# Turns behind the LSTM layer and in the attention layer: from TensorE to 32x32 blocks on VectorE and DMAs, with a new ranking of ready operations

## The chip, the cores and the metric

The kernel runs on one core of a Trainium2 chip, as one program and one launch. The metric is the device time of that program in microseconds. The core's engines run beside each other, each in the order of its own instructions: TensorE (PE in the profile) does matrix products and 128x128 turns (transposes) into PSUM, VectorE (DVE) and ScalarE (ACT) work elementwise, GpSimd (POOL) does small per-row work, and SyncE (SP) issues DMAs. They wait for each other by semaphores.

## The reference

x has 128 batches of 64 nodes with 256 features, which are 8192 rows, all float32. Four layers follow, each as x = layernorm(x + layer(x, adj)):

- Layer 0: three graph convolutions, 256 to 512 to 1024 to 256 features, with the squared entries of adj.
- Layer 1: a spectral layer. The eigenvectors U of a normalised Laplacian turn the nodes, two small products with a relu lie between, and U turns them back.
- Layer 2: two graph convolutions, then LSTMs over windows of 1, 2, 3 and 4 nodes (p = 1 to 4), each of which overwrites the last node of its windows.
- Layer 3: attention among the 64 nodes of a batch.

```
h = x @ W + b_lin                                  # layer 3
scores = (h @ h.T) * graph                         # zeros become -1e16
out = softmax(scores, axis=2) @ h + b
x = layernorm(x + out)
```

## The kernel before

A tile is 128 rows, that is two batches. Four tiles make a group of 512 rows, and there are 16 groups, numbered 0 to 15 in the code (the listing's group variable g). Layer 0 runs first, two groups at a time, with the eigenvector computation woven in; its products are recorded at line 940 and its VectorE work at line 52. Six groups' rows stay in SBUF, ten wait in a DRAM tile called `rest` and are read back when a buffer of X comes free.

Layers 1 to 3 are run by a planner (`Plan`, line 98 on). `unit` (line 1518) notes the work of two groups, or of one for the last four (`SINGLE`), as operations with an engine, an estimated cost, and dependencies. `Plan.run` keeps up to three units going and emits, again and again, the operation that can start earliest. Among operations of one engine that can start within 0.02 us of the earliest, `rank` (line 163) decides: the lower group number goes first, and for TensorE at the very end the group with the most operations left. Emission fixes the order of PE, DVE, ACT and POOL instructions (`manual_schedule`); DMAs on SP are placed by the framework. Buffers are slots by tag: `w` (seven of 128x1024), `v`, `ps` (eight PSUM banks), `gates` and others. `MOST` (line 112) keeps some free slots of each tag for the oldest unit. All instructions that the planner emits are recorded at line 156, so the profile tells them apart by tile name only.

The steps that matter here, by function:

- `turns` (line 1202) notes 128x128 transposes on TensorE: a product with `ident` as one operand, one pass each, where a float32 matrix product makes two instructions.
- `lstm` and `four` (lines 1378 and 1502) keep the state with features on the partitions: hT, in tiles w.
- `from_lstm` (line 1294) copies hT into batch order (VectorE and ScalarE), turns it on TensorE (8 turns a group), and adds half of it to the rows xs, since hT holds twice the hidden state. `norm` (line 1232) then does the layer norm: statistics on VectorE, the inverse root on GpSimd, the scaling on VectorE (on ScalarE for the last two groups, `ENDING`).
- `layer3` (line 1306) turns xs (8 turns a group) to xT, makes hT = xT times dw with the bias dbl on ScalarE, makes the scores, turns hT back to rows hn (8 turns) and adds the bias, takes the softmax without the division, turns e (the tile att, 4 turns), and multiplies eT with hn. The division by the row sum sm comes with the residual.

```
turns([(ps[k][:, cols(t)], xs[:, t, k * P:(k + 1) * P]) for k in range(2)])         # layer3: xT
turns([(p[:, j, c * P:(c + 1) * P], hT[:, c, (t + j) * P:(t + j + 1) * P]) ...])    # layer3: hn
turns([(p[:, t * P:(t + 1) * P], e[:, t, :]) for t in range(nt)])                   # layer3: eT
```

Of the kernel before, what the change touches and what calls it, by code (L numbers as in the profile page):

```python
# [11 lines left out]
F32 = mybir.dt.float32  # L12
# [85 lines left out]


class Op:  # L100
    __slots__ = ("engine", "calls", "cost", "lag", "before", "left", "after", "tiles", "start", "group", "rank", "ready", "unit")


class Plan:
# [4 lines left out]

    LAG = {"PE": 0.205, "DVE": 0.13, "ACT": 0.14, "POOL": 0.0, "SP": 2.0}  # L110

    MOST = {"w": 4, "v": 2, "ps": 4, "gates": 2, "hs": 2}
    OWN = {"PE": 0.0, "DVE": 0.125, "ACT": 0.105, "POOL": 0.0, "SP": 0.0}

    def __init__(self, engines, place, slots):
# [42 lines left out]
    def run(self, units, ways):  # L158
# [4 lines left out]
        def rank(op):  # L163
            if op.engine == "PE" and not todo and len(left) <= LASTS:
                return -left[op.group]
            return op.group or 99

        def candidates(guard):
            oldest = min([u for u in going if u] or [0])
# [22 lines left out]
        while todo or going:  # L192
            while todo and len(going) < ways + (0 in going):
                self.unit, f = todo.pop(0)
                self.ops, self.group = [], 0
                f()
                going[self.unit] = len(self.ops)
                for op in self.ops:
                    left[op.group] = left.get(op.group, 0) + 1
                    if not op.left:  # L200
                        able[op.engine].append(op)
            t, op = (candidates(True) if todo or len(left) > LASTS else None) or candidates(False)
            e = op.engine
            for tile in op.tiles:
                if tile.real is None:
                    s = self.slots[tile.tag]
                    tile.slot, tile.unit = s.index(min(s)), op.unit
                    tile.real = self.place(tile.tag, tile.slot, tile.shape)
                    s[tile.slot] = 1e9
                    held[op.unit, tile.tag] = held.get((op.unit, tile.tag), 0) + 1  # L210
            self.emit(op)
            able[e].remove(op)
            op.start = t
            self.free[e] = t + op.cost
            end = t + op.cost + self.LAG[e]
            for tile in op.tiles:
                tile.left -= 1
                tile.until = max(tile.until, end)
                if not tile.left and tile.slot is not None:
                    self.slots[tile.tag][tile.slot] = tile.until  # L220
                    held[tile.unit, tile.tag] -= 1
            for other in op.after:
                other.ready = max(other.ready, t + op.cost + self.OWN[e] if other.engine == e else end)
                other.left -= 1
                if not other.left:
                    able[other.engine].append(other)
            going[op.unit] -= 1
            left[op.group] -= 1
            if not left[op.group]:
                del left[op.group]  # L230
            if not going[op.unit]:
                del going[op.unit]
# [512 lines left out]
CELLS = 3  # L745
OUTS = 4
LASTS = 3
SINGLE = 4

RING = 6  # L750

# [56 lines left out]
def kernel(  # L808
# [90 lines left out]
    adT2 = keep.tile([P, P], F32, name="adT2")  # L899
    nc.gpsimd.memset(adT2, 0.0)  # L900
    sqT2 = keep.tile([P, P], F32, name="sqT2")
    rs_row = keep.tile([P, P], F32, name="rs_row")
    rs_col = keep.tile([P, 1], F32, name="rs_col")
    u2 = keep.tile([P, P], F32, name="u2")
# [5 lines left out]
    cw1 = load(keep, "cw1", c_w1, "(k p) f -> p k f", [P, 2, D], p=P)  # L910
    dw = load(keep, "dw", d_w, "(k p) f -> p k f", [P, 2, D], p=P)
    dbl = load(keep, "dbl", d_bl, "p (k o) -> p k o", [P, 2, 1], o=1)
    cb1 = keep.tile([P, 2], F32, name="cb1")
    nc.sync.dma_start(cb1, c_b1)
    wide = {}
# [205 lines left out]
    pr = tl(psa, [P, 512], "ps", bufs=6)  # L1121
    PE.matmul(pr[:, :P], ones, adT2, start=True, stop=True)
    V.tensor_copy(rs_row, pr[:, :P])
    V.tensor_reduce(rs_col, adst, AX.X, ALU.add)
    V.tensor_scalar(wide["c_b0"], wide["c_b0"], rs_col, None, op0=ALU.mult)
    V.tensor_add(cbi, cbi, cbh)
    for q in (slice(0, 4), slice(6, 8)):
        V.tensor_scalar(cbi[:, :, q], cbi[:, :, q], 0.5, None, op0=ALU.mult)
    phase_a.close()
# [19 lines left out]
        nc.gpsimd.memset(att[i], 0.0)  # L1149


    def place(tag, slot, shape):
        if tag == "att":
            return att[slot][:, :shape[1], :]
        if tag == "ps":
            return tl(psb, shape, f"ps{slot}")
        if tag in ("w", "v", "gates", "c", "hs"):
# [1 line left out]
        return tl(few, shape, f"{tag}{slot}")  # L1159

    plan = Plan({"PE": nc.tensor, "DVE": nc.vector, "ACT": nc.scalar, "POOL": nc.gpsimd, "SP": nc.sync}, place,
                {"ps": 8, "w": WIDE, "v": 4, "gates": GATES, "c": CELLS, "hs": OUTS, "att": ATT, "mx": 4, "sm": 4, "st": 4, "mv": 4,
                 "rs": 4, "nm": 4})
    V, S, G, Q = (Noted(plan, e) for e in ("DVE", "ACT", "POOL", "SP"))

# [63 lines left out]
        S.copy(dst[:, 1, :], ps[1])  # L1229
        return dst  # L1230

    def norm(x, scalar):
        st, mv, rs = plan.tile("st", [P, 2, 6]), plan.tile("mv", [P, 2, 2]), plan.tile("rs", [P, 2])
        for t in range(2):
            V.bn_stats(st[:, t, :], x[:, t, :])
            V.bn_aggr(mv[:, t, :], st[:, t, :])
        G.tensor_scalar(rs, mv[:, :, 1], EPS, None, op0=ALU.add)
        G.tensor_tensor(rs, rs, half[:, :2], ALU.pow, cost=0.74)
        if scalar:
            nm = plan.tile("nm", [P, 2])  # L1240
# [9 lines left out]
    def layer1(xs):  # L1250
# [14 lines left out]
        for t in range(0, 4, 2):  # L1265
# [1 line left out]
            for j in range(2):  # L1267
                run(p[:, j, :], [(z[:, (t + j) * P:(t + j + 1) * P], bw2)])
            V.tensor_add(xs[:, t:t + 2, :], p, xs[:, t:t + 2, :])
            norm(xs[:, t:t + 2, :], False)  # L1270

    def to_lstm(xs):
        a = mixed(xs, adT2)
        g1 = as3(work(), 4)
        for t in range(0, 4, 2):
            p = ps4((P, 2, D))
# [14 lines left out]
            lstm(hT, p, first, nw)  # L1291
        return hT

    def from_lstm(xs, hT, g):
        hb = as3(work(), 2)
        for bs in (slice(0, 4), slice(4, 8)):
            for k, copy, cost in ((0, V.tensor_copy, 0.33), (1, S.copy, 0.56)):
                copy(as3(hb[:, k, :], 8)[:, bs, :], hT[:, k, :, bs].rearrange("p n b -> p b n"), cost=cost)
        for t in range(0, 4, 2):
            p = ps4((P, 2, D))  # L1300
            turns([(p[:, j, k * P:(k + 1) * P], hb[:, k, (t + j) * P:(t + j + 1) * P]) for j in range(2)
                   for k in range(2)])
            V.scalar_tensor_tensor(xs[:, t:t + 2, :], p, 0.5, xs[:, t:t + 2, :], op0=ALU.mult, op1=ALU.add)
            norm(xs[:, t:t + 2, :], g in ENDING)

    def layer3(xs, g, first, nt):

        tiles = range(first, first + nt)

        def cols(t, n=1):  # L1310
            return slice((t - first) * P, (t - first + n) * P)
# [1 line left out]
        def part(tile, a):  # L1313
            return as3(tile[:, :tile.at.size * nt // 4], a)

        xT = part(work(), 2)
        ps = [ps4() for _ in range(2)]
        for t in tiles:
            turns([(ps[k][:, cols(t)], xs[:, t, k * P:(k + 1) * P]) for k in range(2)])
        if g in ENDING:  # L1320
            S.copy(xT[:, 0, :], ps[0][:, :nt * P])
        else:
            V.tensor_copy(xT[:, 0, :], ps[0][:, :nt * P])
        S.copy(xT[:, 1, :], ps[1][:, :nt * P])
        hT = part(work(), 2)
        for c in range(2):
            p = ps4()[:, :nt * P]
            run(p, [(dw[:, k, c * P:(c + 1) * P], xT[:, k, :]) for k in range(2)])
            S.activation(hT[:, c, :], p, AF.Identity, bias=dbl[:, c, :])
        p = ps4((P, nt, N))  # L1330
        calls = []
        for t in range(nt):
# [11 lines left out]
        mx = plan.tile("mx", [P, 4])[:, :nt]  # L1344
        V.tensor_reduce(mx, s, AX.X, ALU.max)
        V.tensor_sub(s, s, mx.unsqueeze(2).to_broadcast([P, nt, N]))
        e = plan.tile("att", [P, nt, P])
        for h in range(2):
            hs = slice(h * N, (h + 1) * N)
            S.activation(e[hs, :, hs], s[hs, :, :], AF.Exp, cost=0.215 + 0.00042 * nt * N)  # L1350
        hn = part(work(), nt)
        for t in range(0, nt, 2):
            p = ps4((P, 2, D))
            turns([(p[:, j, c * P:(c + 1) * P], hT[:, c, (t + j) * P:(t + j + 1) * P]) for j in range(2)
                   for c in range(2)])

            V.tensor_add(hn[:, t:t + 2, :], p, wide["d_b"].unsqueeze(1).to_broadcast([P, 2, D]))
        sm = plan.tile("sm", [P, 4])[:, :nt]
        p = ps4()[:, :nt * P]
        turns([(p[:, t * P:(t + 1) * P], e[:, t, :]) for t in range(nt)])  # L1360
        eT = work2()[:, :nt * P]
        S.copy(eT, p)
        V.tensor_reduce(sm, e, AX.X, ALU.add)
        V.reciprocal(sm, sm)
        for t in range(0, nt, 2):
            p = ps4((P, 2, D))
            for j in range(2):
                run(p[:, j, :], [(eT[:, (t + j) * P:(t + j + 1) * P], hn[:, t + j, :])])
            x2 = xs[:, first + t:first + t + 2, :]
            for j in range(2):  # L1370
                V.scalar_tensor_tensor(x2[:, j, :], p[:, j, :], sm[:, t + j:t + j + 1], x2[:, j, :],
                                       op0=ALU.mult, op1=ALU.add)
            norm(x2, g in ENDING)
            at = 4 * g + first + t
            for j in range(2):
                Q.dma_start(out_t[:, at + j, :], x2[:, j, :])
# [171 lines left out]
    def left_over():  # L1548
        for piece in norms:
            plan.note("POOL" if piece.__name__ == "root" else "ACT", piece, 0.5, 1.5 * len(plan.ops))  # L1550

    with tc.manual_schedule(engines={mybir.EngineType.PE, mybir.EngineType.DVE, mybir.EngineType.Activation,
                                     mybir.EngineType.Pool}):
# [44 lines left out]
```

## Time and profile before

| what | value |
|---|---|
| median of 3 runs | 2458.52 us (2457.69 to 2458.81) |
| profiled execution, first to last instruction | 2455.8 us |
| between that span and the median | 2.7 us |
| TensorE busy in the 40 slices of the span | 0.9 or more in all but the last |
| granted TensorE clock, mean | 0.998 |
| DMA in the span | 42.69 MB, mean 17 GB/s |

The profiled execution has no time of its own beside its span, so the span is set against the median of the runs. Times are microseconds unless marked ns. In a line of a group the fields are: source line, engine, operation, output tile <- input tiles, shapes, count | busy us, mean ns of one | idle time of the engine in front of it, and what ended most of that. In a timeline the first two numbers are start and length of a run of equal instructions, and brackets hold the idle time before. In a line of stretches the fields are the stretch, its length, the busy time of PE, its weight loads, DVE, ACT and POOL, and then the granted TensorE clock, the DMA share and GB/s. In a line of DMA issues the last number is the median from issue to landing. An instruction's duration holds its latency: on TensorE the next one starts long before it is over, so the pitch between starts is what counts.

### The profile page before, as it was taken

The page shows a single profiled execution, that of the slowest core. Times are in us where ns is not written, and L with a number is a line of the kernel's source. Part 1 is how long each engine was busy: PE and PEld are TensorE (multiplying, and loading weights), DVE is VectorE, ACT ScalarE, POOL GpSimd, SP SyncE. Part 2 cuts the span into 40 slices and gives each one's busy share as a digit, 9 for nine tenths or more (in the row PEclk, how much of TensorE's full clock was granted, in tenths as well). Part 3 has the DMA queues.
Part 4 walks back from the last instruction along what each step waited for, and adds up shares of the span by engine and source line. Part 5 has one row for each costly group of instructions (what it writes and reads, how often), then busy time and mean ns, then how long its engine had stood idle before and what let it go on. Part 6 is the DMA issues. An engine that isn't in the chain of part 4 may idle for free.

```text
span 2455.8 us, 40814 instructions
## 1 busy us (share of the span) xinstructions
PE 2431.6 (99%) x15500; PEld 2158.3 (88%) x15500; DVE 1618.6 (66%) x5676; ACT 1073.0 (44%) x2610; POOL 137.5 (6%) x315
## 2 busy tenths in 40 slices
PE   9999999999999999999999999999999999999997
PEld 7888888878887899989989998998998998988996
DVE  6888877778888265584684486477558458374336
ACT  2333433333333354445444445444444444545555
POOL 0000000000000010010010000001001001010002
PEclk9999999999999999999999999999999999999999
DMA  7000000000000020010000001001001000000000
GB/s 227 9 1 18 9 10 10 9 10 9 9 1 1 35 87 1 1 36 1 1 18 18 1 1 35 1 1 36 1 1 35 1 1 18 1 10 1 1 1 27
DMA packets 27972, 42.69 MB, mean 17 GB/s; under 512 B 2944, under 2 KB 22144, under 8 KB 27776
## 3 DMA queue, kind: packets, MB, share of 16 engines
q1 hardware_dynamic: 27424, 39.81, 4.7%
q8 instruction: 122, 2.00, 0.3%
q14 instruction: 74, 0.61, 0.1%
q10 hardware_dynamic: 352, 0.28, 0.0%
HBM read 26.45 MB, written 13.63 MB: 16 GB/s over the span
## 4 chain that ended last, share of the span: by engine, by line
PE 94%; DVE 4%; DMA 1%; ACT 0%; issue 0%; POOL 0%; SPq 0%; ACTq 0%; POOLq 0%; DVEq 0%
PE ps L156 62%; PE ps L940 31%; DVE D L52 1%; DVE X L156 1%; PE pc L296 1%; DMA XA<-in_x_dram 1%; DVE st L156 0%; DVE tw L52 0%; POOL rs L156 0%; DVE w L156 0%; DVE h L52 0%; ACT gates L156 0%; DVE gates L156 0%; DVE u L52 0%; DVE v L156 0%
## 5 line engine op out<-in xcount | busy, mean ns | idle before, releaser
L156 PE MATMUL ps<-w,wih 128*128 128x128 f32 (+2 forms) x4144 | 752.7, 315 | 0.9 <-DVE gates L156 0.9
L156 PEld LDWEIGHTS ps<-w,wih 128*128 128x128 f32 x4144 | 646.5, 191 | 37.0 <-issue 6.7
L156 ACT ACTIVATE gates<-ps,cbi 128x168 f32<-128x168 f32 (+2 forms) x832 | 342.2, 417 | 361.2 <-PE ps L156 353.0
L156 PE MATMUL ps<-hs,whh 128*128 128x168 f32 (+1 forms) x1952 | 345.1, 291 | 0.0
L156 PEld LDWEIGHTS ps<-hs,whh 128*128 128x128 f32 x1952 | 288.9, 191 | 1.2 <-issue 1.0
L156 PE MATMUL ps<-w,sums 128*128 128x128 f32 x1776 | 237.7, 275 | 0.0
L940 PE MATMUL ps<-aw,h 128*128 128x256 f32 x1024 | 227.2, 379 | 0.0
L156 DVE SCALAR_TENSOR_TENSOR gates<-gates 128x256 f32<-128x256 f32 (+2 forms) x220 | 83.9, 382 | 215.7 <-ACT gates L156 215.1
L156 PEld LDWEIGHTS ps<-w,sums 128*128 128x128 f32 x1776 | 218.1, 192 | 1.5 <-issue 1.2
L940 PEld LDWEIGHTS ps<-aw,h 128*128 128x128 f32 x1024 | 192.9, 190 | 25.9 <-ACT h L949 0.5
L156 ACT ACTIVATE gates<-gates,cbi 128x256 f32<-128x256 f32 x272 | 116.2, 497 | 194.6 <-DVE gates L156 194.6
L949 ACT ACTIVATE h<-h 128x512 f32<-128x512 f32 x128 | 80.4, 629 | 196.3 <-DVE h L52 196.1
L156 DVE TENSOR_TENSOR gates<-gates,ps 128x256 f32<-128x256 f32 x340 | 128.4, 417 | 19.4 <-PE ps L156 14.4
L940 PE MATMUL ps<-ss,tw 128*128 128x256 f32 x512 | 117.9, 380 | 0.0
L940 PE MATMUL ps<-ss,aw 128*128 128x256 f32 x512 | 117.3, 379 | 0.0
L940 PE MATMUL ps<-m,aw 128*128 128x256 f32 x512 | 117.1, 380 | 0.0
L156 DVE SCALAR_TENSOR_TENSOR c<-gates,c 128x256 f32<-128x256 f32 (+2 forms) x156 | 57.1, 366 | 87.2 <-ACT gates L156 87.0
L940 PE MATMUL ps<-aw,m 128*128 128x512 f32 x256 | 114.6, 593 | 0.0
L156 DVE TENSOR_TENSOR gates<-v,ps 128x256 f32<-128x256 f32 x136 | 55.6, 417 | 80.7 <-ACT v L156 49.9
L940 PEld LDWEIGHTS ps<-ss,aw 128*128 128x128 f32 x512 | 96.6, 190 | 12.8
L940 PEld LDWEIGHTS ps<-ss,tw 128*128 128x128 f32 x512 | 96.3, 190 | 12.9 <-issue 0.2
L940 PEld LDWEIGHTS ps<-m,aw 128*128 128x128 f32 x512 | 95.6, 190 | 12.6 <-issue 0.5
(314 smaller groups left out, 3734.7 us busy)
## 6 DMA issues: line engine op xcount, KB each, us to landing
out_dram<-X SPq DMA_DIRECT2D x64, 128.0 KB, 1.8
rest<-XA SPq DMA_DIRECT2D x10, 512.0 KB, 2.6
X<-rest SPq DMA_DIRECT2D x10, 512.0 KB, 3.3
XA<-in_x_dram SPq DMA_DIRECT2D x18, 256.0 KB, 6.0
wih<-in_c_ih_dram SPq DMA_DIRECT2D x4, 1024.0 KB, 7.4
aw<-in_a_w_dram SPq DMA_DIRECT2D x3, 1024.0 KB, 10.8
X<-in_x_dram SPq DMA_DIRECT2D x12, 256.0 KB, 5.9
whh<-in_c_hh_dram SPq DMA_DIRECT2D x3, 1024.0 KB, 9.4
```

The lines of the kernel that those rows point to most:

```text
L52: return getattr(self.engine, name)(out, *args, **kw)
L156: getattr(e, name)(*[real(x) for x in args], **{k: real(v) for k, v in kw.items()})
L296: PE.matmul(out, lhsT, rhs, start=True, stop=True)
L940: PE.matmul(out, lhsT, rhs, start=start, stop=stop)
L949: S.activation(dst, src, AF.Relu)
```

## The change

All groups but the last two stop turning on TensorE behind layer 2 and in layer 3:

- VectorE's `transpose` turns each 32x32 block inside its own 32 partitions and writes the blocks in an order of its own. The new function `across` moves the blocks to their partitions: one DMA writes the 128x1024 tile to a DRAM tile `far` (eight slots), four DMAs read it back, each into 32 partitions.
- This is done for hT behind the LSTM (two VectorE turns a group), for xs (four), and for the hidden rows hn of layer 3 (two). The products read the result through strided views. hn is now a second ScalarE activation with the summed bias dbb = dbl + b, and no longer a biased copy of the turned hT.
- e is turned in one VectorE instruction, and eight DMAs put its blocks straight into the block-diagonal tile att. The exponential is one ScalarE instruction, and the row sum runs over 64 columns a tile and not over 128.
- The factor of a half on hT is gone. Layer 1's norm now gives rows of twice the size (`twice`), so the sum behind the LSTM is twice the old one, and its norm takes four times the eps. The first graph product of layer 2 uses adH2, half of adT2, so layer 2 sees the same values as before.
- The planner computes for each operation the chain that is left behind it in its unit (`tail`), and ranks by `due` = 30 us times the group's number, less that chain. `MOST` for w goes from 4 to 3. The pieces of the layer norms that layer 0 leaves over are chained to each other.

```
-    MOST = {"w": 4, "v": 2, "ps": 4, "gates": 2, "hs": 2}
+    MOST = {"w": 3, "v": 2, "ps": 4, "gates": 2, "hs": 2}
@@ rank
-            return op.group or 99
+            return op.due
@@ run
+                for op in reversed(self.ops):
+                    op.tail = op.cost + max([x.tail + (self.OWN if x.engine == op.engine else self.LAG)[op.engine]
+                                             for x in op.after] or [0.0])
+                    op.due = op.group * PERIOD - op.tail
...
+PERIOD = 30.0
+FARS = 8
...
+    V.tensor_scalar(adH2, adT2, 0.5, None, op0=ALU.mult)
+    V.tensor_add(dbb, dbb, dbl)
...
+    far = [aside.tile([P, 1024], F32, name=f"far{i}") for i in range(FARS)]
@@ to_lstm
-        a = mixed(xs, adT2)
+        a = mixed(xs, adH2)
+    def across(src):
...
+        far = plan.tile("far", [P, 1024])
+        Q.dma_start(far, src, cost=0.6)
+        dst = work()
+        for j in range(4):
+            Q.dma_start(dst[32 * j:32 * j + 32].rearrange("r (i f) -> r i f", i=4),
+                        seen(far[:, 256 * j:256 * j + 256], "(i r) f -> r i f", i=4), cost=0.6)
+        return dst
@@ from_lstm (the last two groups keep the turns)
+        z = work()
+        for k in range(2):
+            V.transpose(z.rearrange("p (j t k f) -> p t j k f", j=4, t=4, k=2)[:, :, :, k],
+                        hT[:, k].rearrange("p n b -> p b n"))
+        y = across(z).rearrange("p (i m f) -> p m i f", i=4, m=8)
         for t in range(0, 4, 2):
-            p = ps4((P, 2, D))
-            turns([(p[:, j, k * P:(k + 1) * P], hb[:, k, (t + j) * P:(t + j + 1) * P]) for j in range(2)
-                   for k in range(2)])
-            V.scalar_tensor_tensor(xs[:, t:t + 2, :], p, 0.5, xs[:, t:t + 2, :], op0=ALU.mult, op1=ALU.add)
-            norm(xs[:, t:t + 2, :], g in ENDING)
+            x2 = xs[:, t:t + 2, :].rearrange("p t (k i f) -> p (t k) i f", k=2, i=4)
+            V.tensor_add(x2, y[:, 2 * t:2 * t + 4], x2)
+            norm(xs[:, t:t + 2, :], False, 4 * EPS)
@@ layer3 (the last two groups keep the turns)
+            z = work()
+            for t in range(0, 4, 2):
+                for k in range(2):
+                    V.transpose(z.rearrange("p (i k t r) -> p t i k r", i=4, k=2, t=4)[:, t:t + 2, :, k],
+                                xs[:, t:t + 2, k * P:(k + 1) * P])
+            xT = across(z).rearrange("p (j k t r) -> p k t j r", j=4, k=2, t=4)
...
             S.activation(hT[:, c, :], p, AF.Identity, bias=dbl[:, c, :])
+            if not ending:
+                h = work2()
+                S.activation(h, p, AF.Identity, bias=dbb[:, c, :])
+                V.transpose(z.rearrange("p (j t c f) -> p t j c f", j=4, t=4, c=2)[:, :, :, c], h)
+        if not ending:
+            hn = across(z).rearrange("p (i t c f) -> p t c i f", i=4, t=4, c=2)
...
+            S.activation(s, s, AF.Exp)
+            V.tensor_reduce(sm, s, AX.X, ALU.add)
+            z = sc.rearrange("p a c -> p (a c)")[:, 256:]
+            V.transpose(z.rearrange("p (b t r) -> p t b r", b=2, t=4), s)
+            for h in range(2):
+                for b in range(2):
+                    for a in range(2):
+                        Q.dma_start(e[64 * h + 32 * b:64 * h + 32 * b + 32, :, 64 * h + 32 * a:64 * h + 32 * a + 32],
+                                    z[64 * h + 32 * a:64 * h + 32 * a + 32, 128 * b:128 * b + 128]
+                                    .rearrange("p (t r) -> p t r", t=4), cost=0.6)
```

More of the change, by code (lines that the diff above doesn't have):

```diff
@@ L100 @@
 class Op:
-    __slots__ = ("engine", "calls", "cost", "lag", "before", "left", "after", "tiles", "start", "group", "rank", "ready", "unit")
+    __slots__ = ("engine", "calls", "cost", "lag", "before", "left", "after", "tiles", "start", "group", "rank", "ready", "unit", "tail", "due")
 class Plan:
     LAG = {"PE": 0.205, "DVE": 0.13, "ACT": 0.14, "POOL": 0.0, "SP": 2.0}
-    MOST = {"w": 4, "v": 2, "ps": 4, "gates": 2, "hs": 2}
+    MOST = {"w": 3, "v": 2, "ps": 4, "gates": 2, "hs": 2}
     OWN = {"PE": 0.0, "DVE": 0.125, "ACT": 0.105, "POOL": 0.0, "SP": 0.0}
@@ L901 @@
     sqT2 = keep.tile([P, P], F32, name="sqT2")
+    adH2 = keep.tile([P, P], F32, name="adH2")
     rs_row = keep.tile([P, P], F32, name="rs_row")
@@ L912 @@
     dbl = load(keep, "dbl", d_bl, "p (k o) -> p k o", [P, 2, 1], o=1)
+    dbb = load(keep, "dbb", d_b, "(k p o) -> p k o", [P, 2, 1], p=P, o=1)
     cb1 = keep.tile([P, 2], F32, name="cb1")
@@ L1154, in place @@
             return att[slot][:, :shape[1], :]
+        if tag == "far":
+            return far[slot]
         if tag == "ps":
@@ L1161 @@
     plan = Plan({"PE": nc.tensor, "DVE": nc.vector, "ACT": nc.scalar, "POOL": nc.gpsimd, "SP": nc.sync}, place,
-                {"ps": 8, "w": WIDE, "v": 4, "gates": GATES, "c": CELLS, "hs": OUTS, "att": ATT, "mx": 4, "sm": 4, "st": 4, "mv": 4,
+                {"ps": 8, "w": WIDE, "v": 4, "gates": GATES, "c": CELLS, "hs": OUTS, "att": ATT, "far": FARS, "mx": 4, "sm": 4, "st": 4, "mv": 4,
                  "rs": 4, "nm": 4})
@@ L1230, in mixed, with norm @@
         return dst
-    def norm(x, scalar):
+    def norm(x, scalar, eps=EPS, twice=False):
         st, mv, rs = plan.tile("st", [P, 2, 6]), plan.tile("mv", [P, 2, 2]), plan.tile("rs", [P, 2])
@@ L1236, in norm @@
             V.bn_aggr(mv[:, t, :], st[:, t, :])
-        G.tensor_scalar(rs, mv[:, :, 1], EPS, None, op0=ALU.add)
+        if twice:
+            G.tensor_scalar(rs, mv[:, :, 1], eps, 0.25, op0=ALU.add, op1=ALU.mult)
+        else:
+            G.tensor_scalar(rs, mv[:, :, 1], eps, None, op0=ALU.add)
         G.tensor_tensor(rs, rs, half[:, :2], ALU.pow, cost=0.74)
@@ L1269, in layer1 @@
             V.tensor_add(xs[:, t:t + 2, :], p, xs[:, t:t + 2, :])
-            norm(xs[:, t:t + 2, :], False)
+            norm(xs[:, t:t + 2, :], False, twice=True)
     def to_lstm(xs):
-        a = mixed(xs, adT2)
+        a = mixed(xs, adH2)
         g1 = as3(work(), 4)
@@ L1292, in to_lstm, with seen @@
         return hT
-    def from_lstm(xs, hT, g):
[L1295 to L1298, printed above, removed]
-        for t in range(0, 4, 2):
-            p = ps4((P, 2, D))
-            turns([(p[:, j, k * P:(k + 1) * P], hb[:, k, (t + j) * P:(t + j + 1) * P]) for j in range(2)
-                   for k in range(2)])
-            V.scalar_tensor_tensor(xs[:, t:t + 2, :], p, 0.5, xs[:, t:t + 2, :], op0=ALU.mult, op1=ALU.add)
-            norm(xs[:, t:t + 2, :], g in ENDING)
+    def across(src):
+        def seen(x, pattern, **kw):
+            return Part(x.tile, x.at, x.rows, x.steps + [("rearrange", (pattern,), kw)])
+        far = plan.tile("far", [P, 1024])
[5 more added lines that the diff above has]
+        return dst
@@ new lines, in from_lstm @@
+    def from_lstm(xs, hT, g):
+        if g in ENDING:
+            hb = as3(work(), 2)
+            for bs in (slice(0, 4), slice(4, 8)):
+                for k, copy, cost in ((0, V.tensor_copy, 0.33), (1, S.copy, 0.56)):
+                    copy(as3(hb[:, k, :], 8)[:, bs, :], hT[:, k, :, bs].rearrange("p n b -> p b n"), cost=cost)
+            for t in range(0, 4, 2):
+                p = ps4((P, 2, D))
+                turns([(p[:, j, k * P:(k + 1) * P], hb[:, k, (t + j) * P:(t + j + 1) * P]) for j in range(2)
+                       for k in range(2)])
+                V.tensor_add(xs[:, t:t + 2, :], p, xs[:, t:t + 2, :])
+                norm(xs[:, t:t + 2, :], True, 4 * EPS)
+            return
+        z = work()
[3 more added lines that the diff above has]
+        y = across(z).rearrange("p (i m f) -> p m i f", i=4, m=8)
+        for t in range(0, 4, 2):
+            x2 = xs[:, t:t + 2, :].rearrange("p t (k i f) -> p (t k) i f", k=2, i=4)
+            V.tensor_add(x2, y[:, 2 * t:2 * t + 4], x2)
+            norm(xs[:, t:t + 2, :], False, 4 * EPS)
@@ L1306, in layer3 @@
     def layer3(xs, g, first, nt):
         tiles = range(first, first + nt)
+        ending = g in ENDING
         def cols(t, n=1):
@@ L1314, in part @@
             return as3(tile[:, :tile.at.size * nt // 4], a)
[L1316 to L1321, printed above, removed]
-        else:
-            V.tensor_copy(xT[:, 0, :], ps[0][:, :nt * P])
-        S.copy(xT[:, 1, :], ps[1][:, :nt * P])
+        if ending:
+            xT = part(work(), 2)
+            ps = [ps4() for _ in range(2)]
+            for t in tiles:
+                turns([(ps[k][:, cols(t)], xs[:, t, k * P:(k + 1) * P]) for k in range(2)])
+            for k in range(2):
+                S.copy(xT[:, k, :], ps[k][:, :nt * P])
+            xT = [xT[:, k, :] for k in range(2)]
+        else:
+            z = work()
+            for t in range(0, 4, 2):
+                for k in range(2):
+                    V.transpose(z.rearrange("p (i k t r) -> p t i k r", i=4, k=2, t=4)[:, t:t + 2, :, k],
+                                xs[:, t:t + 2, k * P:(k + 1) * P])
+            xT = across(z).rearrange("p (j k t r) -> p k t j r", j=4, k=2, t=4)
+            xT = [xT[:, k] for k in range(2)]
         hT = part(work(), 2)
+        z = None if ending else work()
         for c in range(2):
             p = ps4()[:, :nt * P]
-            run(p, [(dw[:, k, c * P:(c + 1) * P], xT[:, k, :]) for k in range(2)])
+            run(p, [(dw[:, k, c * P:(c + 1) * P], xT[k]) for k in range(2)])
             S.activation(hT[:, c, :], p, AF.Identity, bias=dbl[:, c, :])
+            if not ending:
[4 more added lines that the diff above has]
+            hn = across(z).rearrange("p (i t c f) -> p t c i f", i=4, t=4, c=2)
+            hn = [hn[:, t] for t in range(4)]
         p = ps4((P, nt, N))
@@ L1346, in layer3 @@
         V.tensor_sub(s, s, mx.unsqueeze(2).to_broadcast([P, nt, N]))
+        sm = plan.tile("sm", [P, 4])[:, :nt]
         e = plan.tile("att", [P, nt, P])
[L1348 to L1363, printed above, removed]
+        if ending:
+            for h in range(2):
+                hs = slice(h * N, (h + 1) * N)
+                S.activation(e[hs, :, hs], s[hs, :, :], AF.Exp, cost=0.215 + 0.00042 * nt * N)
+            hn = part(work(), nt)
+            for t in range(0, nt, 2):
+                p = ps4((P, 2, D))
+                turns([(p[:, j, c * P:(c + 1) * P], hT[:, c, (t + j) * P:(t + j + 1) * P]) for j in range(2)
+                       for c in range(2)])
+                V.tensor_add(hn[:, t:t + 2, :], p, wide["d_b"].unsqueeze(1).to_broadcast([P, 2, D]))
+            hn = [hn[:, t, :] for t in range(nt)]
+            p = ps4()[:, :nt * P]
+            turns([(p[:, t * P:(t + 1) * P], e[:, t, :]) for t in range(nt)])
+            eT = work2()[:, :nt * P]
+            S.copy(eT, p)
+            eT = [eT[:, t * P:(t + 1) * P] for t in range(nt)]
+            V.tensor_reduce(sm, e, AX.X, ALU.add)
+        else:
+            S.activation(s, s, AF.Exp)
+            V.tensor_reduce(sm, s, AX.X, ALU.add)
+            z = sc.rearrange("p a c -> p (a c)")[:, 256:]
+            V.transpose(z.rearrange("p (b t r) -> p t b r", b=2, t=4), s)
+            for h in range(2):
+                for b in range(2):
[3 more added lines that the diff above has]
+                                    .rearrange("p (t r) -> p t r", t=4), cost=0.6)
+            eT = [e[:, t, :] for t in range(nt)]
@@ L1367, in layer3 @@
             for j in range(2):
-                run(p[:, j, :], [(eT[:, (t + j) * P:(t + j + 1) * P], hn[:, t + j, :])])
+                run(p[:, j, :], [(eT[t + j], hn[t + j])])
             x2 = xs[:, first + t:first + t + 2, :]
@@ L1372, in layer3 @@
                                        op0=ALU.mult, op1=ALU.add)
-            norm(x2, g in ENDING)
+            norm(x2, ending)
             at = 4 * g + first + t
@@ L1550, in left_over @@
             plan.note("POOL" if piece.__name__ == "root" else "ACT", piece, 0.5, 1.5 * len(plan.ops))
+            for first, then in zip(plan.ops[-2:], plan.ops[-1:] if len(plan.ops) > 1 else []):
+                first.after.append(then)
+                then.before.add(first)
+                then.left += 1
     with tc.manual_schedule(engines={mybir.EngineType.PE, mybir.EngineType.DVE, mybir.EngineType.Activation,
```

## The prediction

> **What bounds the kernel now.** The page comes first: its parts 1, 2 and 4.
>
> ```profile
> span 2455.8 us, 40814 instructions
> PE 2431.6 (99%) x15500; PEld 2158.3 (88%) x15500; DVE 1618.6 (66%) x5676; ACT 1073.0 (44%) x2610; POOL 137.5 (6%) x315
> ...
> PE   9999999999999999999999999999999999999997
> ...
> PE 94%; DVE 4%; DMA 1%; ACT 0%; issue 0%; POOL 0%; SPq 0%; ACTq 0%; POOLq 0%; DVEq 0%
> ```
>
> TensorE is the bound almost without a gap: it idles 24.2 us in all, 5.5 before the first data and 15.9 after 2400 us. VectorE and ScalarE have room. So a TensorE instruction removed is worth its pitch, and a wait that reaches TensorE costs its whole length. The groups of TensorE by tile give what the change removes most of:
>
> ```profile
> L156 PE MATMUL ps<-ident,w 128*128 128x128 f32 x256 | 35.0, 277 | 0.4 <-ACT w L156 0.3
> L156 PE MATMUL ps<-ident,X 128*128 128x128 f32 x128 | 18.3, 274 | 1.3 <-ACT X L156 1.3
> L156 PE MATMUL ps<-ident,att 128*128 128x128 f32 x64 | 10.0, 277 | 0.7 <-ACT att L156 0.5
> ```
>
> Those are 448 turns, 28 in each of 16 groups. The 277 ns is one turn's latency, not its pitch. The pitch comes from TensorE's timeline, which also shows the way from the LSTM into layer 3 in one pair of groups (1056.97 is its last LSTM product, 1071.38 its first product with dw):
>
> ```profile
> 1056.97 0.39 PE L156 MATMUL ps<-w,whh 128*128 128x128 f32 x2
> 1057.20 1.88 PE L156 MATMUL ps<-w,cw 128*128 128x512 f32 x4
> ...
> 1071.38 3.60 PE L156 MATMUL ps<-w,dw 128*128 128x512 f32 x8
> ...
> 2404.76 1.91 PE L156 MATMUL ps<-ident,w 128*128 128x128 f32 x16
> 2406.51 0.61 PE L156 MATMUL ps<-w,wih 128*128 128x128 f32 x4
> ```
>
> Sixteen turns take 2406.51 - 2404.76 = 1.75 us: 0.109 each. In the same way a half product of 128, 256 or 512 columns takes 0.11, 0.215 or 0.43. From 1057.20 to 1071.38 pass 14.2 us in which TensorE is never idle: other groups' products lie there. The same stretch on VectorE and GpSimd:
>
> ```profile
> 1061.29 0.48 DVE L156 SCALAR_TENSOR_TENSOR w<-gates 128x128 f32<-128x128 f32 x2
> 1061.70 1.28 DVE L156 TENSOR_TENSOR X<-ps,X 128x512 f32<-128x512 f32 x2
> 1062.90 0.74 DVE L156 BATCH_NORM_STATS2 st<-X 128x6 f32<-128x256 f32 x2
> 1067.51 1.54 DVE L156 TENSOR_SCALAR X<-X,mv,rs 128x256 f32<-128x256 f32 x4
> ```
>
> ```profile
> 1066.05 0.22 POOL L156 TENSOR_SCALAR rs<-mv 128x2 f32<-128x2 f32 x1 [90.13 <-DVE mv L156]
> 1066.35 0.70 POOL L156 TENSOR_TENSOR rs<-rs,half 128x2 f32<-128x2 f32 x1
> ```
>
> The last of hT is written at 1061.77, 4.6 us after the last LSTM product. Last, the DMA issues:
>
> ```profile
> out_dram<-X SPq DMA_DIRECT2D x64, 128.0 KB, 1.8
> rest<-XA SPq DMA_DIRECT2D x10, 512.0 KB, 2.6
> X<-rest SPq DMA_DIRECT2D x10, 512.0 KB, 3.3
> ```
>
> **What goes.** In 14 of 16 groups all 28 turns go: 392 x 0.109 = 42.7 us of TensorE, all on the path. Nothing is added there. That the moving operands become strided blocks costs nothing by a row: products that read hT in strides take 379 ns at 256 columns, like those on the contiguous h of layer 0.
>
> **What comes beside it, at nothing.** Per changed group VectorE loses two copies of 256 (388 ns), one of 512 (683), two adds (686) and half a reduce (0.3), and gains four block turns of 512 and five of 256. No row shows a block turn. Straight copies (683 and about 410) make it 4.8 - 3.1 = 1.7 us more; ScalarE's rearranged write (1137 ns against 628 straight) is the upper row and makes it 5.5. I take the copy, since VectorE's own rearranged copy of 256 took 388, no more than a straight one. 14 x 1.7 = 24 us lie in VectorE's 840 idle us. ScalarE loses 1.6 us a group. SP issues 23 more DMAs a group (3 x 5 through DRAM, 8 for att) at 333 ns: 7.7 us per group of some 100, with 3 MB. The one-off work (adH2, dbb, scales folded into norm) is under 1 us. MOST for w 4 to 3 and the chained left-over norms move only order.
>
> A rule speaks against the move: the Trainium skill, VectorE: DVE Perf Modes, Rules for kernel authors, sends a 128x128 turn to TensorE where PSUM will do. By that rule alone this change makes the kernel slower. The rows speak for the move as far as its latency is covered: TensorE is at 99%, VectorE at 66%.
>
> **What comes on the path.** The turns cost latency. A pass through DRAM (call it a hop) is a 512 KB write, 2.6, then four 128 KB reads issued 0.33 apart, the last landing about 1.8 after its issue, and 0.5 of wake-ups: 2.6 + 1.0 + 1.8 + 0.5 = 5.9, say 6.0. Ends: 5.3 without wake-ups and with landings of 1.7; 8.3 if four issues take 3.05, as four of out_dram once did on the queue's timeline, and the last lands in 2.7, the longest of out_dram. The queue is in order: behind the waiting reads of one group stand the other group's reads, the att blocks, outputs and the reload of X. Two more engines now wait for DMAs: VectorE's adds of the turned hT, with the next groups' gate operations behind them, and TensorE's dw product, with all of TensorE behind it.
>
> From a pair's last LSTM product to its first dw product the new chain is 4.6 (to hT) + 1.3 (two block turns) + 6.0 + 1.3 (adds) + 1.8 (statistics) + 2.2 (two rounds of GpSimd) + 0.8 (scaling the last pair) + 1.4 (four block turns) + 6.0 = 25.4 us, against at most 14.2 before; some of it overlaps, so 25. Against it stands what the changed order gives TensorE. I counted the products between the same two places in its instruction order, at the pitches above: 23.0, 21.3, 20.3, 22.8, 20.3 and 17.3 us in the six pairs (before, 13 to 14). The shortfalls are 2.0, 3.7, 4.7, 2.2, 4.7 and 7.7: **25 us of new TensorE waits**. Every microsecond on one hop adds 12. With hops of 5.3 the sum is 17; with 8.3 it is 52. Block turns at the upper row would add 2.2 us to each chain, 13 in all.
>
> The pair's second group has 33 to 42 us of products and is covered. From the scores to the att product the chain is about 10 us (softmax on VectorE 2.7 and its DMAs, queued behind hn's write and reads) against 10.6 to 12: I add 3 us for all of these, at most 20 if issues are slow.
>
> **The end.** Groups 14 and 15 keep their turns, but group 13 does not, and the order runs it beside them. Before, 44.8 us pass from the last LSTM product (2411.0) to the end. After it group 13 needs 1.5 + 1.3 + 6.0 + 1.3 + 1.8 + 2.2 + 0.8 + 1.4 + 6.0 = 22.3 to its dw products, 5.5 to its scores done, 10 to att, 7 for product, norm and output: 44.8, and shares VectorE with two other groups. I take 49: +4, from 0 to +10.
>
> **Ranking** by remaining chain moves which product comes next. On a bound engine an order costs nothing until it leaves nothing to run; that is counted above.
>
> **The clock** is the open risk of waits over 3 us:
>
> ```profile
> 2440.00:2444.00 4.00, 2.57 (x12) 1.91 (x11) 4.00 (x16) 0.00 (x1) 0.80 (x2) 1.00 0.00 0
> 2444.00:2448.00 4.00, 0.00 (x0) 0.00 (x0) 4.00 (x17) 0.00 (x0) 1.75 (x5) 0.77 0.29 97
> 2448.00:2452.00 4.00, 0.00 (x0) 0.00 (x0) 0.82 (x4) 2.18 (x4) 3.21 (x11) 0.50 0.31 105
> ```
>
> The granted clock (third from the right) falls to half some 3.6 us after TensorE's last product at 2442.6 (a mean of 0.77 over 2444 to 2448 puts the step at 2446.2). Four waits here are that long. No row shows what a return costs, so I put it at 0 to 2 us each and take 0 in the sum. The Trainium skill, TensorE: Matmul & The Clock Gate, Part 1, asks for about 3.4 us of busy time before full clock returns; by that the sum would be some 7 us higher.
>
> **Sum**, against the profiled execution's span: 2455.8 - 42.7 + 25 + 3 + 4 = 2445.1. The median of the runs is 2.7 above the span, and the waits of VectorE for DMAs, which stall other groups behind them in order, add an estimated 1: **2449 us**.
>
> **Rivals.** *The gain arrives almost whole* (chance 0.2): hops near 5.3, parts of the chain overlapping, under 17 us of waits: 2425 to 2440. For it: DMA is idle (its row shows zeros over most of the span). Against it: the covers are counted, and the chain's rows are measured.
>
> *Slower* (0.33): one mechanism, the hop. If it takes 8.3 us, through slow issue of small blocks or reads that queue behind the other group's on SP, the waits are 52 and TensorE gives back more than it was spared: 2449 + 27 = 2476. It breaks even at about 6.8 us a hop and passes 0.2% slower at 7.2. For it: four small issues once took 3.05 us, and the reads are 1 KB blocks into 32 partitions, smaller than any large transfer here. Against it: 128 KB landed in 1.8.
>
> *It doesn't do what it says*, turns left on TensorE: the changed order holds 56 turns of groups where 448 were, so this is out (0.0).
>
> **How the numbers follow.** 0.2% of 2458.5 is 4.9 us, about what a measurement of this kernel tells from no change. The likeliest case, waits of 17 to 35 us, spans 2440 to 2460 and has 0.47: 0.3 of it below 2453.6, 0.17 inside. With the full gain, faster is 0.5; same is 0.17 + 0.01 from the slow case; slower 0.32. The range runs from the middle of the full-gain case, 2432, to the slow case's price, 2480.
>
> **What would show it.** Right: TensorE busy about 2389 us, "ps<-ident" down to 32, 16 and 8 instructions, a new wait of TensorE for a DMA into w (dw) in six places of 2 to 8 us, far writes landing near 2.6, block turns near 0.68 and 0.41. Wrong: no such waits, or hops far from 6 us, TensorE's idle time near 24, or waits of LSTM products for VectorE instead.

## The result and the profile after

The changed kernel takes 2512.28 us (median, 2508.63 to 2514.53) against 2458.66 beside it: a ratio of 1.0218, 95% interval 1.0204 to 1.0232. It is slower, by 53.6 us, and lies above the prediction's range of 2432 to 2480. The profiled execution took 2508.63 with a span of 2506.8, 51.0 above the span before.

The page after, parts 1, 2 and 4 (span; busy us of each engine; TensorE's 40 slices; the chain that ended last):

```profile
span 2506.8 us, 40722 instructions
PE 2413.5 (96%) x15108; PEld 2133.2 (85%) x15108; DVE 1647.0 (66%) x5734; ACT 1042.0 (42%) x2568; POOL 137.1 (5%) x315
...
PE   9999999999999999989989999998998998999996
...
PE 84%; DVE 7%; DMA 4%; SPq 2%; ACT 2%; issue 1%; POOL 1%; ACTq 0%; DVEq 0%; POOLq 0%
```

392 products are gone (15500 to 15108), but TensorE's busy time fell by only 18.1 us and its idle time rose from 24.2 to 93.3. Before, 94% of the chain was TensorE; now 16% of it is others. TensorE's waits after (releaser, total us, times, longest):

```profile
PE ps L156 <- DVE hs L156: 18.5, 6, 7.7
PE ps L156 <- DMA w<-far: 14.5, 7, 3.2
PE ps L156 <- DVE w L156: 14.2, 11, 3.7
PE ps L156 <- DMA X<-rest: 8.9, 2, 6.0
PE ps L156 <- ACT X L156: 6.8, 1, 6.8
```

The forecast wait for a DMA into w is there, in seven places, yet it is not the largest. TensorE waits longer for VectorE, for hs (the state that one LSTM step hands to the next) and for w (a work buffer, here mostly the input of an LSTM product). Nearly all of these belong to groups that are still in the LSTM, and their own chain up to there holds no hop. The two lines make 32.7 us; before, there was none for hs and this one for w:

```profile
PE ps L156 <- DVE w L156: 1.0, 3, 0.4
```

VectorE's own longest wait for a DMA shows what stands in front of them (its list of waits, same columns):

```profile
DVE X L156 <- DMA w<-far: 24.8, 8, 4.8
```

Seven of these eight waits are followed within 10 us by a wait of TensorE for hs or w, 24.9 us in all of the 32.7.

The DMA issues of the hops (count, KB each, median us from issue to landing):

```profile
far<-w SPq DMA_DIRECT2D x42, 512.0 KB, 2.6
w<-far SPq DMA_DIRECT2D x168, 128.0 KB, 3.1
```

And VectorE's groups of block turns (busy us, mean ns of one):

```profile
L156 DVE STREAM_TRANSPOSE w<-w 128x512 f32<-128x512 f32 x28 | 29.8, 1091 | 0.1
L156 DVE STREAM_TRANSPOSE w<-X 128x256 f32<-128x256 f32 x56 | 20.1, 412 | 0.9 <-PE ps L156 0.9
L156 DVE STREAM_TRANSPOSE w<-v 128x512 f32<-128x512 f32 x28 | 19.9, 710 | 24.3 <-ACT v L156 15.8 <-PE ps L156 8.3
```

The timeline of the first pair of groups shows how, VectorE first, then the two waits of TensorE that follow (start, length, [idle before <- releaser]):

```profile
1082.83 1.29 DVE L156 TENSOR_TENSOR X<-w,X 128x512 f32<-128x512 f32 x2 [2.38 <-DMA w<-far]
1084.04 1.40 DVE L156 BATCH_NORM_STATS2 st<-X 128x6 f32<-128x256 f32 x4
...
1086.28 1.28 DVE L156 TENSOR_TENSOR X<-w,X 128x512 f32<-128x512 f32 x2
1087.56 1.54 DVE L156 TENSOR_SCALAR X<-X,mv,rs 128x256 f32<-128x256 f32 x4
1089.02 1.42 DVE L156 STREAM_TRANSPOSE w<-X 128x256 f32<-128x256 f32 x4
1090.36 0.72 DVE L156 SCALAR_TENSOR_TENSOR hs<-gates 128x256 f32<-128x256 f32 x2
```

```profile
1090.80 0.49 PE L156 MATMUL ps<-hs,whh 128*128 128x128 f32 x2 [2.49 <-DVE hs L156]
1098.19 1.10 PE L156 MATMUL ps<-w,dw 128*128 128x512 f32 x2 [2.44 <-DMA w<-far]
```

VectorE waits for the turned hT, and the adds, norm and next block turns of the old pair stand in its order ahead of hs of the younger pair. TensorE runs dry at 1088.3 for want of hs, and again at 1095.75 for the second hop. The hops took 8.6 us here (last block turn done 1074.25, add at 1082.83) and 7.8 (1090.4 to 1098.19).

**Where 51.0 us come from.** Idle +69.1; removed turns -42.7; TensorE at half clock +19.8 (TensorE's busy time times the missing share of the clock, summed over stretches of 4 us; before, 0.0). That makes 46.2; 4.8 are left; products that start alone, and so show their latency, may be the cause, but no run tests it. TensorE's listed waits grew by 72.5 us: 34.5 for tiles that VectorE writes (hs, w, gates, c: 36.4 against 1.9), 14.5 for the dw products, 8.9 for the reload of X, 12.0 for tiles of ScalarE, most of it at the end, and 2.2 for att.

### The profile page after: what moved, and what is told of

The parts are those of the page before. It is cut to its first block, busy times and chain, and to the rows that moved or that the text cites. A ratio compares the mean times of both kernels' runs of the same rounds, so it can differ in the third digit from the quotient of the medians.

```text
span 2506.8 us, 40722 instructions
## 1 busy us (share of the span) xinstructions
PE 2413.5 (96%) x15108; PEld 2133.2 (85%) x15108; DVE 1647.0 (66%) x5734; ACT 1042.0 (42%) x2568; POOL 137.1 (5%) x315
## 3 DMA queue, kind: packets, MB, share of 16 engines
q1 hardware_dynamic: 74064, 85.70, 10.8%
## 4 chain that ended last, share of the span: by engine, by line
PE 84%; DVE 7%; DMA 4%; SPq 2%; ACT 2%; issue 1%; POOL 1%; ACTq 0%; DVEq 0%; POOLq 0%
PE ps L156 52%; PE ps L948 31%; DMA w<-far 2%; DVE w L156 2%; SPq L156 1%; DVE X L156 1%; ACT gates L156 1%; DMA far<-w 1%; POOL rs L156 1%; DVE D L52 1%; DVE gates L156 1%; DVE st L156 1%; PE pc L300 1%; DMA XA<-in_x_dram 1%; DVE tw L52 0%
## 5 line engine op out<-in xcount | busy, mean ns | idle before, releaser
L156 PE MATMUL ps<-w,wih 128*128 128x168 f32 (+2 forms) x4144 | 757.9, 317 | 13.9 <-DVE w L156 11.9
L156 PEld LDWEIGHTS ps<-w,wih 128*128 128x128 f32 x4144 | 651.0, 192 | 55.8 <-DVE w L156 12.5
L156 PE MATMUL ps<-hs,whh 128*128 128x168 f32 (+1 forms) x1952 | 343.0, 293 | 18.6 <-DVE hs L156 18.5
L156 PE MATMUL ps<-w,sums 128*128 128x128 f32 x1776 | 231.9, 275 | 0.0
L156 POOL TENSOR_SCALAR rs<-mv 128x2 f32<-128x2 f32 x96 | 23.9, 259 | 1518.7 <-DVE mv L156 1517.8
```

Of the source, the lines that this page charges most:

```text
L156: getattr(e, name)(*[real(x) for x in args], **{k: real(v) for k, v in kw.items()})
```

## The experiments

The first theory after the result: the two hops between the LSTM and dw cost the time, above all since VectorE waits in order. The rivals: the new ranking alone; every hop, wherever it stands; later, VectorE's added work, too few ready operations, and an order made for shorter hops. Every ratio is to the kernel before, run beside it (medians 2457.2 to 2458.4).

**rank_only** puts the new ranking on the kernel before:

```
-            return op.group or 99      # before
+            return op.due              # and MOST w 3, chained left-over norms
```

> The kernel before with the new ranking, MOST of 3 and the chained left-over norms, and all turns on TensorE as before. Theory A (the loss comes from the two hops between the LSTM and the dw product, where VectorE waits in order for a DMA and holds up the younger units): ranking alone costs little, 2455 to 2470 us. Theory B (the loss is the new order): 2480 us or more, since the new order alone would leave TensorE without work.

It took 2465.96 us, ratio 1.0036 (1.0022 to 1.0050). The ranking, with the MOST of 3 and the chained norms that come with it, costs 8.8 us by itself. The prediction had all three at nothing.

**old_rank** undoes those three in the changed kernel.

> The changed kernel with the old ranking (lower group first), MOST of 4 and unchained left-over norms. Theory A: the block turns cost as much or more, 2500 to 2550 us. Theory B: the loss goes away, 2425 to 2455 us.

It took 2540.52 us, ratio 1.0339 (1.0323 to 1.0354): the block turns without the ranking are worse by 28 us. So the ranking is not the cause of the loss; it softens what the turns bring and costs 8.8 where there are none.

**late_only** and **early_only** split the turns:

```
-        if g in ENDING:                 # from_lstm; the same condition for xT in layer3
+        if g in ENDING or not EARLY:    # late_only: EARLY False
-        if ending:                      # hn and e in layer3
+        if ending or not LATE:          # early_only: LATE False
```

> The changed kernel with only hn and e turned by blocks; hT behind the LSTM and xs in layer 3 are turned on TensorE again (16 turns a group, 224 in all, 24.4 us at 0.109). Theory A: the chain from the LSTM to dw has no hop, and the 168 turns that are still gone are worth 18.3 us, of which some 3 to 8 go into waits for hn and att: 2442 to 2452 us. Theory B: 2490 or more. Theory C (every hop costs about the same, whatever stands around it; after loses 42.7 + 54 = 96 us over 42 hops and 14 rounds of att): about 2458 - 18 + 14 x 2.3 = 2472 us.

> The changed kernel with only hT behind the LSTM and xs in layer 3 turned by blocks (224 turns gone, 24.4 us); hn and e are turned on TensorE. Theory A: nearly all of the new waits are still there, 2500 to 2520 us. Theory C: two thirds of the loss, 2458 - 24 + 14 x 4.6 = 2498 us. Theory B: as after, 2500 or more.

late_only took 2458.83 us (1.0006, 0.9997 to 1.0015), early_only 2520.66 (1.0257, 1.0242 to 1.0273). The late turns (hn, e) lose nothing: late_only is 7.1 us below rank_only, though above the 2452 expected. The early ones (hT, xs) carry the whole loss: early_only is 54.7 us above rank_only. That every hop costs alike is out.

**late_old** is late_only with the old ranking.

> hn and e turned by blocks as in late_only, with the old ranking, MOST of 4 and unchained left-over norms. If the ranking costs the same with these turns as with the old ones (8.8 us), 2458.8 - 8.8 = 2450, between 2445 and 2453. If the block turns need the new ranking, as the whole change does (2541 without it against 2512 with it), 2460 or more.

It took 2468.55 us (1.0043, 1.0031 to 1.0056): a miss. TensorE's waits hold one of 6.0 us for att's DMAs and, 10 us ahead of it, one of 5.2 at another att product, for which the trace names no cause. I read them as an order that counted on the blocks earlier than they came; no run shows this by itself.

**no_y** and **no_x** each put one of the early turns back on TensorE.

> The changed kernel with hT behind the LSTM turned on TensorE again; xs, hn and e stay by blocks, so one hop is left between the LSTM and dw, and VectorE waits for no DMA there. 280 turns are gone, 30.5 us. If VectorE waiting in order for the first hop, with the younger units' hs behind it, is the larger part: 2445 to 2475 us. If TensorE's wait for the second hop is the larger part: 2490 to 2510 us.

> The changed kernel with xs in layer 3 turned on TensorE again; hT behind the LSTM, hn and e stay by blocks (280 turns gone, 30.5 us), so only the first of the two hops between the LSTM and dw is left. If the cause is the sum of two hops in series, which one alone would not overrun: about what no_y took, 2465 to 2480 us. If it is VectorE that waits in order for the first hop with the younger units' hs behind it: 2490 to 2505 us.

no_y (second hop left) took 2472.91 us (1.0061, 1.0047 to 1.0075), no_x (first hop left) 2506.78 (1.0198, 1.0184 to 1.0212), a little above what was expected for it. With as many turns saved (280), the hop that VectorE waits for costs 34 us more than the one that TensorE waits for, each in the order that the planner gave it. Two hops in series are not needed for the loss.

**hop_act** takes the latency out of all hops, **y_act** out of the first alone (on no_x):

```
-        far = plan.tile("far", [P, 1024])     # and the five DMAs
+        dst = work()
+        S.copy(dst, src)
+        return dst
```

> The changed kernel in which a hop is one ScalarE copy of 128x1024 (about 1 us) in place of the five DMAs through DRAM; the blocks do not change partitions, so the values are wrong. Block turns, adds and e's DMAs stay. If the latency of the DMAs is the cause: the 42.7 us of turns are won, less 9 for the ranking and up to 10 for the end and att: 2422 to 2435 us. If VectorE's added work or the new order is the cause, its waits stay: 2470 or more.

> no_x with the first hop (hT behind the LSTM) as one ScalarE copy of about 1 us in place of the five DMAs; the blocks of hT do not change partitions, so the values are wrong. VectorE's block turns and adds stay. If the DMA latency is what costs: 8 turns a group (12.2 us) less than late_only's 2459 and some waits more, 2447 to 2468 us. If VectorE's added work costs: 2485 or more.

hop_act took 2471.09 us (1.0052, 1.0036 to 1.0067), y_act 2466.75 (1.0037, 1.0024 to 1.0050). Some 40 us of the loss go with the latency in either, but hop_act does not come near the 2422 to 2435 that the latency as sole cause would give. hop_act's waits of TensorE hold five new ones, at dw:

```profile
PE ps L156 <- ACT w L156: 28.9, 5, 6.1
```

The first of them in its timeline:

```profile
1086.54 5.83 PE L156 MATMUL ps<-w,dw 128*128 128x512 f32 x8 [5.53 <-ACT w L156]
```

The planner now counts about 1 us for the hop and puts dw earlier, ahead of what could fill the gap. The likely reason that dw is late again is the chain on VectorE, with block turns every 1.04 us that the planner costs at 0.60. After the wait these eight products take 5.83 us where they take 3.6 at full clock.

**true_cost** tells the planner of a lag of 3.0 us on each DMA, and of the block turns' true costs.

> The changed kernel whose planner is told what the trace shows: a lag of 3.0 us in place of 2.0 on each DMA, 1.04 us for a strided block turn of 512 and 0.66 for a straight one, in place of 0.60. If the loss comes from a plan that counts on shorter hops, 2470 to 2495 us. If there is not enough other work to lie under the two hops, whatever the plan knows: 2500 us or more.

It took 2498.08 us (1.0163, 1.0149 to 1.0176): 14 us back, between the two expectations. The planner now counts 9.0 us for a hop (0.6 + 3.0 + 4 x 0.6 + 3.0), more than the 7.8 to 8.6 measured. The waits for hs fell from 18.5 to 12.5, and others came, among them one of 11.2 us for att.

**all_w8** adds an eighth w buffer to such a plan (lag 2.6).

> The whole change with an eighth w buffer (WIDE 8), and a planner told of a DMA lag of 2.6 us in place of 2.0, 1.04 us for a strided block turn of 512 and 0.66 for a straight one. If the hops overrun because too few operations of other groups are ready (seven w buffers hold three units back), one more buffer brings back more than the true costs alone did (2498): 2465 to 2485 us. If the hops cannot be covered whatever is ready: 2490 or more.

It took 2501.78 us (1.0180, 1.0166 to 1.0194): a miss. More buffers for other groups do not bring the time back.

**y_planned** leaves hop, work and buffers of no_x as they are and tells the planner of 3 us more on the first hop alone:

```
-        Q.dma_start(far, src, cost=0.6)
+        Q.dma_start(far, src, cost=0.6 + more)     # more = 3.0 for the turned hT, else 0
```

> no_x with the hop as it is, and a planner that counts 3 us more for it, so that VectorE's adds stand later in its order. If the loss comes from adds that stand ahead of younger units' ready work and wait there: 2465 to 2488 us. If the latency itself is on the path, whatever the order: 2500 or more.

It took 2459.58 us (1.0008, 0.9998 to 1.0018): 47 us less than no_x, with the same instructions, by the planner's order alone (and the buffer slots that follow from it). VectorE's added work is the same in both, so it is not what cost these 47 us. VectorE in the same place as shown above for the changed kernel:

```profile
1082.89 1.29 DVE L156 TENSOR_TENSOR X<-w,X 128x512 f32<-128x512 f32 x2 [0.98 <-DMA w<-far]
...
1086.01 0.41 DVE L156 SCALAR_TENSOR_TENSOR hs<-gates 128x256 f32<-128x256 f32 x1
```

In no_x hs comes behind them:

```profile
1088.63 0.76 DVE L156 SCALAR_TENSOR_TENSOR hs<-gates 128x256 f32<-128x256 f32 x2
```

The blocks land at about the same time, but in y_planned hs stands ahead of the second group's adds and of the scaling: it is begun at 1086.0, against 1088.6 in no_x and 1090.4 in the changed kernel. VectorE's waits for these DMAs in no_x and then in y_planned:

```profile
DVE X L156 <- DMA w<-far: 26.5, 8, 5.7
DVE X L156 <- DMA w<-far: 8.8, 7, 3.9
```

TensorE's waits for tiles of VectorE (w, X, hs, gates) fall from 32.2 to 16.6, and those for the reload of X from 12.2 to none: the unit before it ends its outputs in time.

**all_planned** is the whole change, with 2 us more planned for both early hops and PERIOD 36.

> The whole change, with a planner that counts 2 us more for each of the two hops between the LSTM and dw, and a PERIOD of 36 in place of 30 (with 30 the plan finds no free w buffer). All 392 turns stay on VectorE; buffers as in the change. If the order made for too short hops is the cause: 2455 to 2480 us, 30 us or more under the change. If two hops in series overrun the other work whatever the order: 2495 or more.

It took 2467.94 us (1.0041, 1.0027 to 1.0055): 44 us of the 53.6 are back, with all 392 turns on VectorE, every hop through DRAM and as many buffers. This run changes PERIOD too, and PERIOD was not run alone; y_planned has no such second edit. The planner counts 9.0 us for each early hop here, as it did in true_cost, which got only 14 us back. So the other 30 us hang on what else differs between the two: PERIOD, the planned lag of all other DMAs, the step of the hop that is given the extra time, and the planned cost of the block turns. These were not tried apart.

**late_w8** is the version that the runs pointed to, only hn and e by blocks under the old ranking, and **before_w8** its control:

```
-WIDE = 7
+WIDE = 8        # both; also MOST w 3 and a planned DMA lag of 2.8 in place of 2.0
```

> Only hn and e by blocks, old ranking, WIDE 8, MOST of 3 for w and a planned DMA lag of 2.8 us. late_old lost its gain at two places where att's blocks came late (6.0 and 5.2 us); with more buffers and later att products these should go: 2458 - 18 + 5 = 2445, between 2441 and 2451 us, faster than both kernels. If late turns cost what they bring: 2455 to 2462 us.

> Control for late_w8: the kernel before, with WIDE 8, MOST of 3 for w and a planned DMA lag of 2.8 us, all turns on TensorE. If these three numbers alone made late_w8 faster, this is faster too, 2450 or less. If the turns do it: 2455 to 2468 us.

WIDE is the number of w buffers. late_w8 takes 2446.72 us, ratio 0.9953 (0.9940 to 0.9965): faster than both kernels. before_w8 takes 2463.40 (1.0025, 1.0016 to 1.0034). So the planner's numbers do not make it faster; against its control the late turns are worth 16.7 us of the 18.3 that they remove. Against the kernel before the gain is 10.8. The page of late_w8:

```profile
span 2444.9 us, 40856 instructions
PE 2417.9 (99%) x15332; PEld 2142.2 (88%) x15332; DVE 1617.4 (66%) x5692; ACT 1074.6 (44%) x2610; POOL 135.9 (6%) x315
```

TensorE idles 27.0 us, nearly as little as before, and waits 1.8 for att's DMAs. Which of the buffer, MOST and the lag took late_old's waits away was not tried apart.

## Why the prediction was wrong

The direction was wrong, and so was the size. By its own steps:

- **What goes, 42.7 us: right.** The turn groups stand at 32, 16 and 8 instructions, as foretold. TensorE's busy time came out at 2413.5 and not 2389, of which 19.8 is half clock.
- **The hop, 6.0 us (5.3 to 8.3): too short.** It took 8.6 and 7.8 in the pair above. The write landed in 2.6 as forecast. Four reads took 1.78 us to issue and not 1.3 (eight, for both groups, took 4.22), and they landed in 3.1 (median) and not 1.8. The bound of 8.3 was nearly met, but the price on it, 2476, was not: the measured time lies 36 above it.
- **Block turns: right but for one.** 0.71 and 0.41 against 0.68 and 0.41 for contiguous sources; the turn of hT, which reads and writes in strides, took 1.09, near the upper row (1.14). The reason for taking the lower one, VectorE's rearranged copy, did not hold for it.
- **New waits at dw, 25 us: they are 14.5,** 1.8 of it in the end. TensorE came later to these products, since it had already waited for hs and w.
- **VectorE's waits that stall other groups, "an estimated 1": this is the step that failed.** The prediction named the wait and what was queued behind it, and put 1 us on it without working it out. Tiles written by VectorE cost TensorE 34.5 us more than before, and 24.9 of TensorE's waits for hs and w come right behind a wait of VectorE for a hop. no_x against no_y sets the hop behind which VectorE waits at 34 us over the other.
- **Ranking, MOST and the chained norms, 0: 8.8 us** by rank_only.
- **The clock, 0 in the sum: 19.8 us**, at nine places where four were named. What failed was the count of waits. The price of one return can be read: behind a wait of 6.0 us that ended at 1165.18 the clock is back at about 1168.6 (0.92 in the stretch from 1168 to 1172). The Trainium skill, TensorE: Matmul & The Clock Gate, Part 1, asks for about 3.4 us of busy time, and this return agrees with it. The stretches behind that wait (the clock is third from the right):

```profile
1160.00:1164.00 4.00, 0.00 (x0) 0.00 (x0) 3.93 (x13) 1.12 (x1) 2.41 (x4) 0.73 0.52 170
1164.00:1168.00 4.00, 2.82 (x13) 2.85 (x14) 0.32 (x1) 0.00 (x0) 0.00 (x0) 0.50 0.12 47
1168.00:1172.00 4.00, 4.00 (x21) 3.61 (x21) 0.87 (x3) 1.98 (x5) 0.00 (x0) 0.92 0.01 4
```

- **That wait of 6.0 us is for the reload of X**, whose DMA is issued only when the unit before has issued its outputs (1158.48 to 1160.3, the reload at 1161.83). The prediction named the reload there and left it out of the sum: 8.9 us in two places, none before.
- **The end, +4 (0 to 10): +11.0.** From the last LSTM product to the end pass 55.8 us, 44.8 before.
- **Scores to att, +3: 2.2,** about as forecast.

The deeper fault lies under all of these. The prediction priced a chain against the products beside it and took the instruction order as given. The order comes from a planner that counts 7.0 us for a hop (0.6 + 2.0 + 4 x 0.6 + 2.0) that takes 7.8 to 8.6, and 0.60 for a turn of 1.04. In an order made for shorter steps, engines wait at one instruction while others behind it are ready. Shown: the order alone moves 47 us (y_planned), and a changed plan moves 44 us (all_planned, with PERIOD). Not shown: that the measured cost is the right number to plan with, since true_cost, which plans with nearly that, got 14 us back, and y_planned counts 10.0 for its hop. The latency by itself is no sufficient cause: with it and a plan that counts on it the time is 2468 (all_planned) and 2460 (y_planned); without it and with a plan that counts on about 1 us it is 2471 (hop_act) and 2467 (y_act). What stays open is the rest of all_planned, 10.5 us above the kernel before: 8.8 is what the ranking cost on the old turns, and its TensorE still waits 10.8 us for att and 6.6 for X.

The rule that spoke against the change (the Trainium skill, VectorE: DVE Perf Modes, Rules for kernel authors) sends a turn of 128x128 to TensorE. For the turn of hT it is borne out here: with a fitting order the move brings nothing (y_planned 2459.58 against late_only's 2458.83, though 112 more turns, 12.2 us, are gone). For xs no run tries the move alone under such an order. For the late turns the measurement goes against the rule: 16.7 us gained against the control.

## What to carry to other kernels

Before a DMA is put into a dependency chain, look for the engine that will wait for it in order: its price is what is queued behind the waiting instruction, not the hop less its cover. Where a planner sets the order, a new step's planned cost belongs to the change: measure the step in a trace, and try more than one planned cost before judging the idea, since here 3 us more on one hop brought 47 us back and nearly true costs on every step brought 14. Move first the steps whose result is needed late: the two turns with slack behind them (hn, e) were worth almost all that they removed, and hT's turn, needed at once, nothing.

## What the runs showed of the hardware

- Reads of 128 KB back from DRAM into 32 partitions landed in 3.1 us (median of 168), while writes of 128 KB to the output landed in 1.8 (median of 64). Four of the reads took 1.78 us to issue.
- A VectorE block turn of 128x512 float32 takes 0.71 us from a contiguous source and 1.09 in the strided form.
- The granted clock did not fall by the length of TensorE's wait alone. In the changed kernel, behind waits of 2.76 and 3.18 us (ending at 1293.08 and 1299.88) it read 1.00; behind one of 2.86 (ending at 1372.10) it read 0.68 over the next 4 us. No run here says why.
